# Where a turned tile's slots lie in PSUM, when the layer-2 inputs are loaded, and when lent adjacency tiles return: three edits in a four-layer graph network on one Trainium2 core

## The chip, the cores and the metric

The kernel runs on one core of one Trainium2 chip. The metric is the device time of one execution in microseconds (us); three runs give a median. The engines are named as in the profile: PE (TensorE; PEld its weight loads), DVE (VectorE), ACT (ScalarE), POOL (GpSimd) and SP (SyncE, which here only issues DMAs). ACT and POOL issue DMAs as well.

## What is computed

Four graph layers run one after the other on x (8 batches, 2048 nodes, 64 features), each followed by a residual sum and a layer norm. In short:

```python
# layer 0: hyperedge attention over H (2048 nodes x 64 edges) and a graph product
agg    = einsum('ben,bnf->bef', softmax(masked s), h)         # per hyperedge
all_he = elu(beta * h + (1 - beta) * agg)                     # per node and edge
g      = einsum('bne,benf->bnf', softmax(masked se), all_he)
industry = einsum('nm,bmf->bnf', adj / deg, x @ W_ind)
out    = mix of (industry, g) by a softmax of tanh(f @ fcW + fcb) @ av
# layer 1: normalized adjacency
H = einsum('bmd,nm->bnd', X, D^-1/2 (A + I) D^-1/2);  out = H @ W.T
# layer 2: adaptive graph convolution, supports I, adj, 2 adj adj - I and
#          apt = softmax(relu(emb @ emb.T)); weights per node from emb and weights_pool
# layer 3: three steps of a gated propagation over adj (adj_matrix), weights W1, W2
```

## The kernel before

**Layout.** Nodes lie in 16 tiles of 128 (NT) or 4 chunks of 512 (NCH, chunk c). Batches go in 4 pairs (NP, pair p). Matrix products with exact inputs are done as two matmuls, one with a rounded high part (v0h) and one with the remainder (v0l); `split` cuts them, the high part on ACT (L167) and the low part on DVE (L168). All 16 adjacency tiles stay on the core; 8 of them, 7 to 14 (LEND = 7, LENT = 8), lie in two lent blocks `adj_more`, which are written to HBM (adj_hbm) before layer 2's slots need the room, and are read back at the opening of layer 3 (`return_adj`, L1681).

**Layer 0, slot loop** (L799 to L832, 80 to 221 us). A node belongs to few hyperedges: tile t has as many "slots" as `SLOT_TILES = [16, 15, 10, 6, 3, 1, 1, ...]` has entries over t: twelve for tile 0, five for the next two, then four, three and two. For each slot PE sums pz out of three matmuls, DVE scales it (L816), ACT takes the exponential, DVE and POOL add up. `begin(t)` gathers a tile's factors into `ps`, a PSUM bank of its own (of its 512 columns 192 are used). `slots(t, ...)` turns the slot numbers of the tile after next (transpose `pslot`, two ACT copies L288) in a buffer of the rotating set "mm", which the pz tiles use too (three buffers).

**Filler.** `fill(n)` takes n matmuls out of a generator: first `products()`, the products of layer 0 with the adjacency, and then `layer1(0)` to `layer1(3)`. It is called between the steps of the slot loop (`fill(3)`, `fill(5)`) and of the mix loop, so that PE has work while other engines prepare the next step. `tick()` counts the filler matmuls; `after(n, f)` and `later(n, f)` place f that many ticks further on in the program. Where layer 1 needs a part that the program has not yet cut at that point, the generator yields "wait" and no matmul; `fill` then only ticks.

**Mix loop** (L1086 to L1105, 226 to 456 us, 16 steps i = 4p + c). A step is mix_scores, mix_end of the step before, mix_ind and mix_g of the next, and mix_weigh, each followed by fill(8) or fill(9). `mix_end` transposes (pt), normalizes and stores x1 (L971); `l1_parts(p, c)` loads it back (L992), scales it on POOL (L995) and splits it into the part that `layer1(p)` multiplies for tiles 4c to 4c + 3.

**Layer 1's end.** After each half g of a pair, `layer1` copies its two sums on ACT (ut, L1058); `l1_end` multiplies by the weights (po), normalizes and, for pairs 0 to 2, stores into x2_hbm. Once all four chunks of a pair are done and `room` is set, `load_xn` places the load of layer 2's xn[p] on ACT's queue, 14 ticks later (L1033). The instructions in `pin(...)` keep their program order on their engine; the x loads of L1033 are not pinned.

**Layers 2 and 3** follow: apt (508 to 747), the supports, 32 slots of formed weights and multiplications (to 1243), and layer 3. In slot 32 (SLOTS) the last chunk's sums are picked (DVE, L1548); then `store` sends y (L1584) and loads xb (L1590), `load` reads y back (L1596), DVE adds and normalizes (L1602, L1618), and `first_turn(3)` transposes the last quarter (pt). `load_first(NT - 4, NT - 2)` (L1634) loads tiles 12 and 13 of x from HBM.

Of the kernel before, what the change touches and what calls it, by code (L numbers as in the profile page):

```python
# [56 lines left out]
def tile_gnn_fast(  # L57
# [199 lines left out]
    def column_halves(a):  # L257
        return [a[:, cols(g, N // 2)] for g in range(2)]

    def lent_tiles():  # L260

        tiles = []
        for i in range(2):
            more = adj_pool.tile([P, LENT // 2, N], F32R, tag=f"more{i}", name="adj_more")
            tiles += [column_halves(more[:, k, :]) for k in range(LENT // 2)]
        return tiles

    adj = [adj_tile(adj_pool, t) for t in range(LEND)] + lent_tiles()

    hrows = {}  # L270

# [9 lines left out]

    def slots(t, psum, tag, bufs):

        pt = psum.tile([E, P], F32, tag=tag, name="pslot", bufs=bufs)
        transpose(pt, hrows[t][:, BF + 8:])
        slot = hy.tile([P, P], BF16, tag="slot", name="slot", bufs=2)
        for i in range(2):
            nc.scalar.copy(slot[i * E:(i + 1) * E, :], pt)  # L288
        one_hot[t] = []
        for s in range(sum(n > t for n in SLOT_TILES)):  # L290
            o = hrp.tile([P, P], F32R, tag="o", name="o", bufs=17)
            if t == 0:
                tc.keep_in_program_order(
                    nc.vector.tensor_scalar(o, slot, float(s + 1), None, op0=ALU.is_equal)
                )
            else:

                far = hy.tile([P, P], BF16, tag="far", name="far", bufs=2)
                nc.scalar.activation(far, slot, AF.Abs, bias=number[:, s:s + 1])
                nc.scalar.activation(o, far, AF.Relu, bias=1.0, scale=-1.0)  # L300
            one_hot[t].append(o)
# [463 lines left out]
    with ExitStack() as pb_scope:  # L765
        pps = pb_scope.enter_context(tc.tile_pool(name="pb_ps", bufs=1, space=PSUM))
        places["small"] = lambda shape, name: pps.tile(shape, F32, tag="mm", name=name, bufs=3)
        pl = pb_scope.enter_context(tc.tile_pool(name="pl", bufs=1))

        def begin(t):  # L770

            k = tiles.index(t)
            for ahead in tiles[k + 2:k + 4]:
                fetch_rows(ahead)
            hrow = hrows.pop(t)
            both = split(hrp, hrow[:, 0:BF], "hr", 2, [P, BF], nc.vector if t == 0 else nc.gpsimd, t == 0)
            ohs = one_hot.pop(t)
            S = len(ohs)
            ps = pps.tile([P, 12, 2, B], F32, tag="ps", name="ps", bufs=1)
            for s, o in enumerate(ohs):  # L780
                mm(ps[:, s].rearrange("p i b -> p (i b)"), lhsT=o, rhs=ts2, start=True, stop=True)

            R = pl.tile([P, 13, B], F32, tag="R", name="R", bufs=2)
            nc.vector.tensor_tensor(
                R[:, 0:S], ps[:, 0:S, 0, :], hrow[:, None, BF:BF + 8].to_broadcast([P, S, B]), ALU.add
            )
            nc.vector.tensor_reduce(R[:, S], ps[:, 0:S, 1, :].rearrange("p s b -> p b s"), AX.X, ALU.add)
            nc.vector.reciprocal(R[:, 0:S + 1], R[:, 0:S + 1])
            co = pl.tile([P, 12, B], F32, tag="co", name="co", bufs=2)
            nc.vector.tensor_tensor(  # L790
                co[:, 0:S], ps[:, 0:S, 1, :], R[:, S:S + 1, :].to_broadcast([P, S, B]), ALU.mult
            )
            return S, both, ohs, R, co


        tiles = [*range(NT - 2), NT - 1, NT - 2]
        now = begin(0)
        slots(tiles[1], pps, "mm", 3)
        for k, t in enumerate(tiles):  # L799
            S, both, ohs, R, co = now  # L800
            acc = pl.tile([P, B, F], F32, tag="acc", name="acc", bufs=2)
            for s in range(S):
                pz = pps.tile([P, C], F32, tag="mm", name="pz", bufs=3)
                for i, (l, r) in enumerate(((ident_r, both[0]), (ident_r, both[1]), (ohs[s], tab2))):
                    mm(pz, lhsT=l, rhs=r, start=i == 0, stop=i == 2)
                if s == 0 and k + 1 < NT:
                    fill(3)
                    now = begin(tiles[k + 1])
                fill(5)
                for _ in range(2):  # L810
                    if to_load:
                        load_adj(*to_load.pop(0))
                if s == max(0, S - 5) and k + 2 < NT:
                    slots(tiles[k + 2], pps, "mm", 3)
                z = pz.rearrange("p (b f) -> p b f", f=F)
                nc.vector.tensor_tensor(z, z, R[:, s, :, None].to_broadcast([P, B, F]), ALU.mult)  # L816
                y = pl.tile([P, B, F], F32, tag="y", name="y", bufs=3)
                nc.scalar.activation(y, z, AF.Exp, bias=-1.0)

                nc.vector.scalar_tensor_tensor(y, z, 1.0, y, op0=ALU.max, op1=ALU.min)  # L820
                cb = co[:, s, :, None].to_broadcast([P, B, F])
                if s == 0:
                    nc.vector.tensor_tensor(acc, y, cb, ALU.mult)
                else:
                    nc.vector.tensor_tensor(y, y, cb, ALU.mult)
                    nc.gpsimd.tensor_tensor(acc, acc, y, ALU.add)

            nc.gpsimd.indirect_dma_start(
                out=gs_hbm[:], out_offset=bass.IndirectOffsetOnAxis(ap=order[:, t:t + 1], axis=0),
                in_=acc.rearrange("p b f -> p (b f)"), in_offset=None,  # L830
            )
# [193 lines left out]

    room = []

    def load_xn():

        for p in range(NP - 1):  # L1030
            if room and done[p] == NCH:
                done[p] = 0
                after(14, lambda p=p: nc.scalar.dma_start(xn[p], x2_hbm[p][:]))  # L1033

    def layer1(p):

        for g in range(2):
            own = (2 * g, 2 * g + 1)
            ug = None
            for t in range(NT):  # L1040
                while (p, t // JT) not in part:
                    yield "wait"
                if ug is None:
                    ug = pph.tile([P, 2, C], F32, tag="ph", name="u1", bufs=2)
                    u = {c: ug[:, c % 2, :] for c in own}
                for i in range(2):
                    for c in own:
                        mm(
                            u[c], lhsT=part[p, t // JT][i][:, t % JT, :], rhs=adj_c(t, c),
                            start=t == 0 and i == 0, stop=t == NT - 1 and i == 1,  # L1050
                        )
                        tick()
                        yield
                if g == 1 and p + 1 < NP and t % JT == JT - 1:
                    l1_parts(p + 1, t // JT)
            for k, c in enumerate(own):
                ut = va.tile([P, C], F32, tag="ut", name="ut", bufs=2)
                pin(nc.scalar.copy(ut, u[c]))  # L1058
                later(6 + 8 * k, lambda p=p, c=c, ut=ut, x1=l1_load(p, c): l1_end(p, c, ut, x1))

    def all_pairs():
        yield from remaining
# [592 lines left out]

    at(SLOTS - 3, 0, first_tiles)
    at(SLOTS, 0, lambda: [first_turn(q) for q in range(3)])
    at(SLOTS, 2, lambda: load_first(NT - 4, NT - 2))
    for q in range(2):
        at(SLOTS, 1 + q, lambda q=q: factor(q, h[q], bd_e, None, True))  # L1660

    for g in range(1, SLOTS + 1):
        for period in range(4):
            for f in hooks.pop((g, period), ()):
                f()
            if 0 < g < SLOTS:
                form(g, 2 * period)
                form(g, 2 * period + 1)
            for f in picks[:2]:
                f()  # L1670
            del picks[:2]
            if g > 0:
                multiply(g - 1, period)
            if g == SLOTS:
                for f in picks:
                    f()
                picks.clear()
    store, load, *waiting = ends[-1]
    adj[LEND:LEND + LENT] = lent_tiles()

    def return_adj(tiles, eng):  # L1681
        for t in tiles:
            for g in range(2):
                pin(eng.dma_start(adj[t][g].bitcast(F32), adj_hbm[t - LEND, :, cols(g, N // 2)]))

    return_adj(range(LEND, LEND + LENT // 2), nc.gpsimd)
    store()
    load()
    return_adj(range(LEND + LENT // 2, LEND + LENT), nc.sync)


# [985 lines left out]
```

## Time and profile before

| what | value |
|---|---|
| runs | 1728.06, 1728.79, 1730.58 us; median 1728.79 |
| profiled execution | 1730.81 us; its span 1729.0, 1.8 lie around it |
| mean granted PE clock | 0.989 |
| PE busy | 1655.4 us, 96% of the span |
| DVE, ACT, POOL busy | 843.0, 589.1, 569.9 us |
| 99 to 221 us (slot loop) | PE 107.68, DVE 113.79 of 122 us |
| 242 to 454 us (mix loop) | PE 210.73, DVE 148.08 of 212 us |
| 484 to 492 us (layer 1's end) | PE 4.75 of 8 us at clock 0.57 |
| 1262 to 1275 us (layer 3's opening) | PE 7.61 of 13 us at clock 0.87 |

A row of a timeline shows start, duration, engine, line, operation, output and input, count, and in brackets the idle time before it with the instruction that ended it. A row of the waits shows who waited for whom, microseconds in total, times, and the longest one. PE's matmuls are pipelined, so their rows overlap; distances between starts are read for what one costs (one filler matmul of 512 columns: 0.233 us).

### The profile page before, as it was taken

Reading aid. Unit: us, or ns where it says so; the run is one execution under the profiler, and the core shown is the slowest. Engines: PE = TensorE matmul, PEld = TensorE weight load, DVE = VectorE, ACT = ScalarE, POOL = GpSimd, SP = SyncE. Lnnn points to the kernel's source line nnn. Section 1 sums busy time; section 2 is a strip of 40 time slices with the busy share of each in tenths; the row PEclk is TensorE's granted clock in tenths of the full one; section 3 lists DMA queues with packets and bytes.
Section 4 is the critical chain, followed back from the end, with each engine's and each line's share of the span. In section 5 each row is a group of like instructions: output and inputs, shape, how many; then the busy total and the mean of one; then the engine's idle time right before and its main releaser. Section 6 shows DMA issues by size and latency. Waiting matters only on the chain. (4 is left out here: it accounts for less than half of the span.)

```text
span 1729.0 us, 28043 instructions
## 1 busy us (share of the span) xinstructions
PE 1655.4 (96%) x11230; PEld 1208.0 (70%) x11230; DVE 843.0 (49%) x1536; ACT 589.1 (34%) x1033; POOL 569.9 (33%) x516
## 2 busy tenths in 40 slices
PE   6888899999989999999999999999989999999996
PEld 4666666666664444478888778888767877878775
DVE  7789945768742221210136157777533433433332
ACT  1355533344321212111213267878511221212221
POOL 3678845556534543422123001313210200202001
PEclk9899999999999999999999999999999999999998
DMA  9833334444330000027344457675571111211111
GB/s 341 277 134 125 121 131 138 146 147 146 117 118 1 31 31 1 24 71 296 113 134 140 118 137 158 138 168 126 171 242 48 50 55 43 62 48 42 57 43 39
DMA packets 171212, 195.83 MB, mean 113 GB/s; under 512 B 71568, under 2 KB 116368, under 8 KB 169792
## 3 DMA queue, kind: packets, MB, share of 16 engines
q1 hardware_dynamic: 160384, 154.61, 30.3%
q0 software_dynamic: 8544, 30.68, 5.3%
q10 hardware_dynamic: 2144, 8.65, 1.3%
q8 instruction: 90, 1.47, 0.4%
q14 instruction: 50, 0.41, 0.1%
HBM read 126.72 MB, written 67.17 MB: 112 GB/s over the span
## 5 line engine op out<-in xcount | busy, mean ns | idle before, releaser
L172 PE MATMUL ua<-pt,xn 128*128 128x512 f32 x512 | 230.2, 592 | 1.4 <-DVE pt L1177 1.4
L172 PEld LDWEIGHTS ua<-pt,xn 128*128 128x128 f32 x512 | 97.0, 190 | 111.0 <-issue 104.1
L1542 DVE COPY w_half<-pw 128x512 f32<-128x512 f32 x160 | 109.8, 705 | 87.8 <-PE pw L172 87.1
L1538 ACT COPY w_half<-pw 128x1024 f32<-128x1024 f32 x128 | 129.8, 1014 | 58.6 <-PE pw L172 58.5
L172 PE MATMUL py<-w_half,xg 128*32 128x128 f32 x4096 | 142.1, 279 | 3.1 <-issue 3.1
L172 PE MATMUL u<-adj,v0h 128*128 128x512 f32 (+1 forms) x388 | 135.7, 427 | 0.6 <-ACT h L1856 0.6
L172 PE MATMUL u<-adj,v0l 128*128 128x512 f32 (+1 forms) x388 | 125.8, 402 | 0.0
L172 PE MATMUL u<-adj_more,v2h 128*128 128x512 f32 (+1 forms) x388 | 125.7, 402 | 0.0
L172 PEld LDWEIGHTS py<-w_half,xg 128*32 128x32 f32 x4096 | 111.3, 138 | 20.5 <-issue 3.7
L172 PE MATMUL u<-adj_more,v2l 128*128 128x512 f32 (+1 forms) x388 | 124.0, 396 | 0.0
L1183 POOL TENSOR_TENSOR acc<-acc,pt 128x512 f32<-128x512 f32 x60 | 76.4, 1274 | 104.3 <-DVE pt L1177 103.7
L172 PE MATMUL pw<-est,wst 64*128 64x256 f32 x1024 | 109.8, 317 | 0.5 <-ACT w_half L1538 0.4
L1177 DVE TENSOR_SCALAR pt<-pt 128x512 f32<-128x512 f32 x64 | 29.8, 465 | 152.8 <-ACT pt L1176 152.7
L172 PEld LDWEIGHTS pw<-est,wst 64*128 64x128 f32 x1024 | 82.2, 185 | 25.4 <-ACT w_half L1538 18.7
L1757 ACT CAST ar<-fcav 128x512 fp32r<-128x512 f32 x64 | 39.6, 618 | 165.7 <-DMA fcav<-in_adj_t 164.8
L172 PE MATMUL u<-adj_more,v3l 128*128 128x512 f32 (+1 forms) x291 | 93.5, 396 | 2.1 <-DVE v3l L168 2.0
L1758 DVE SCALAR_TENSOR_TENSOR ar<-fcav,ar 128x512 f32<-128x512 f32 x64 | 45.6, 713 | 100.6 <-ACT ar L1757 100.6
L1176 ACT ACTIVATE pt<-s 128x512 f32<-128x512 f32 x64 | 38.0, 598 | 164.8 <-PE s L172 164.8
L172 PE MATMUL u<-adj,v1h 128*128 128x512 f32 (+1 forms) x291 | 94.0, 401 | 0.0
L172 PE MATMUL u<-adj_more,v3h 128*128 128x512 f32 (+1 forms) x291 | 93.1, 398 | 0.0
L172 PE MATMUL u<-adj,v1l 128*128 128x512 f32 (+1 forms) x291 | 92.6, 395 | 0.0
L1727 POOL TENSOR_TENSOR x<-x,rows 128x512 f32<-128x512 f32 x16 | 22.5, 1431 | 211.8 <-PE pt L175 200.5
(409 smaller groups left out, 3288.4 us busy)
## 6 DMA issues: line engine op xcount, KB each, us to landing
fcav<-in_adj_t SPq DMA_DIRECT2D x64, 256.0 KB, 2.9
u_hbm<-ut SPq DMA_DIRECT2D x48, 256.0 KB, 2.8
xg<-u_hbm SPq DMA_DIRECT2D x24, 512.0 KB, 7.0
adj<-in_adj_t POOLq DMA_DIRECT2D x16, 512.0 KB, 7.9
adj_more<-in_adj_t POOLq DMA_DIRECT2D x16, 512.0 KB, 7.9
adj_hbm<-adj_more SPq DMA_DIRECT2D x16, 512.0 KB, 6.1
x_hbm<-r SPq DMA_DIRECT2D x28, 256.0 KB, 2.3
hs_hbm<-st ACTq DMA_DIRECT2D x8, 584.0 KB, 5.9
```

The lines of the kernel that those rows point to most:

```text
L172: tc.keep_in_program_order(nc.tensor.matmul(*args, **kw))
L1176: nc.scalar.activation(pt, s, AF.Exp)
L1177: nc.vector.tensor_scalar(pt, pt, 1.0, None, op0=ALU.max)
L1183: nc.gpsimd.tensor_tensor(accs[c], accs[c], pt, ALU.add)
L1538: pin(nc.scalar.copy(dst, pw.rearrange("p j o n -> p n (j o)")))
L1542: pin(copy(dst[:, :, 2 * j:2 * j + 2], bank.rearrange("p o n -> p n o")))
L1727: nc.gpsimd.tensor_tensor(xs, xs, b2.to_broadcast([P, JT, P]), ALU.add)
L1757: nc.scalar.copy(ar, seen_a)
L1758: nc.vector.scalar_tensor_tensor(ar.bitcast(F32), seen_a, 1.0, ar.bitcast(F32), op0=ALU.mult, op1=ALU.not_equal, accum_out=left[:, t, k:k ...
```

## The change

1. **Slots.** The bank of `ps` becomes one persistent tile `shared`. For a tile with over six slots (only tile 0 has them, k = 0) the slot numbers of the tile after next are turned into its columns 384 to 511; for the others they go to an "mm" buffer as before, and `fill(4)` follows: for k = 1 to 13, 52 matmuls in all.
2. **x loads.** `load_xn` no longer places L1033's loads by ticks but collects them; `begin_loads()` issues them, on ACT's queue as before, behind the two ut copies at the end of a half of `layer1`; after the last half they are issued at once.
3. **Adjacency return.** Tiles 7 to 10 are read back on SP at the start of slot 32, in place of POOL's queue behind the slot; tiles 11 to 14 stay on SP behind `store` and `load`. `load_first(NT - 4, NT - 2)` moves from period 2 of slot 32 to behind `load`.

```diff
     def slots(t, psum, tag, bufs):
-        pt = psum.tile([E, P], F32, tag=tag, name="pslot", bufs=bufs)
+        pt = psum.tile([E, P], F32, tag=tag, name="pslot", bufs=bufs) if tag else psum
...
+        shared = pps.tile([P, C], F32, tag="ps", name="ps", bufs=1)
...
-            ps = pps.tile([P, 12, 2, B], F32, tag="ps", name="ps", bufs=1)
+            ps = shared[:, 0:24 * B].rearrange("p (s i b) -> p s i b", i=2, b=B)
...
                 if s == max(0, S - 5) and k + 2 < NT:
-                    slots(tiles[k + 2], pps, "mm", 3)
+                    if S > 6:
+                        slots(tiles[k + 2], shared[0:E, C - P:C], None, 1)
+                    else:
+                        slots(tiles[k + 2], pps, "mm", 3)
+                        fill(4)
...
+    xn_loads, at_once = [], []
+
+    def begin_loads():
+        while xn_loads:
+            p = xn_loads.pop(0)
+            nc.scalar.dma_start(xn[p], x2_hbm[p][:])
+
     def load_xn():
         for p in range(NP - 1):
             if room and done[p] == NCH:
                 done[p] = 0
-                after(14, lambda p=p: nc.scalar.dma_start(xn[p], x2_hbm[p][:]))
+                xn_loads.append(p)
+        if at_once:
+            begin_loads()
...
                 later(6 + 8 * k, lambda p=p, c=c, ut=ut, x1=l1_load(p, c): l1_end(p, c, ut, x1))
+            if (p, g) == (NP - 1, 1):
+                at_once.append(True)
+            begin_loads()
...
-    at(SLOTS, 2, lambda: load_first(NT - 4, NT - 2))
...
+    def return_first():
+        adj[LEND:LEND + LENT // 2] = lent_tiles(0)
+        return_adj(range(LEND, LEND + LENT // 2), nc.sync)
+
+    at(SLOTS, 0, return_first)
...
     store, load, *waiting = ends[-1]
-    adj[LEND:LEND + LENT] = lent_tiles()
...
-    return_adj(range(LEND, LEND + LENT // 2), nc.gpsimd)
+    adj[LEND + LENT // 2:LEND + LENT] = lent_tiles(1)
     store()
     load()
+    load_first(NT - 4, NT - 2)
     return_adj(range(LEND + LENT // 2, LEND + LENT), nc.sync)
```

`lent_tiles(i)` now makes one of the two lent blocks; `return_adj` itself is unchanged and moved up in the text.

More of the change, by code (lines that the diff above doesn't have):

```diff
@@ L258, in column_halves, with lent_tiles @@
         return [a[:, cols(g, N // 2)] for g in range(2)]
[L260 to L268, printed above, removed]
+    def lent_tiles(i):
+        more = adj_pool.tile([P, LENT // 2, N], F32R, tag=f"more{i}", name="adj_more")
+        return [column_halves(more[:, k, :]) for k in range(LENT // 2)]
+    adj = [adj_tile(adj_pool, t) for t in range(LEND)] + lent_tiles(0) + lent_tiles(1)
     hrows = {}
@@ L1657, in tile_gnn_fast, with return_adj @@
     at(SLOTS, 0, lambda: [first_turn(q) for q in range(3)])
-    at(SLOTS, 2, lambda: load_first(NT - 4, NT - 2))
     for q in range(2):
         at(SLOTS, 1 + q, lambda q=q: factor(q, h[q], bd_e, None, True))
+    def return_adj(tiles, eng):
+        for t in tiles:
+            for g in range(2):
+                pin(eng.dma_start(adj[t][g].bitcast(F32), adj_hbm[t - LEND, :, cols(g, N // 2)]))
+    def return_first():
+        adj[LEND:LEND + LENT // 2] = lent_tiles(0)
+        return_adj(range(LEND, LEND + LENT // 2), nc.sync)
+    at(SLOTS, 0, return_first)
     for g in range(1, SLOTS + 1):
@@ L1678, in tile_gnn_fast @@
     store, load, *waiting = ends[-1]
-    adj[LEND:LEND + LENT] = lent_tiles()
[L1681 to L1684, printed above, removed]
-    return_adj(range(LEND, LEND + LENT // 2), nc.gpsimd)
+    adj[LEND + LENT // 2:LEND + LENT] = lent_tiles(1)
     store()
     load()
+    load_first(NT - 4, NT - 2)
     return_adj(range(LEND + LENT // 2, LEND + LENT), nc.sync)
```

## The prediction

> **What bounds the kernel now.** The page comes first: TensorE (PE) is busy for 96% of the span, so only PE's idle time (1729.0 − 1655.4 = 73.6 us) and matmuls at a reduced clock can be won; no matmul is removed. The change touches three stretches, read by windows, waits and timelines.
>
> ```profile
> PE 1655.4 (96%) x11230; PEld 1208.0 (70%) x11230; DVE 843.0 (49%) x1536; ACT 589.1 (34%) x1033; POOL 569.9 (33%) x516
> ```
>
> Busy time by window (columns PE, PEld, DVE, ACT, POOL, then PE's clock, DMA share, GB/s):
>
> ```profile
> 110.00:123.00 13.00, 11.77 (x53) 8.83 (x53) 12.85 (x25) 7.00 (x19) 9.71 (x8) 1.00 0.14 44
> 182.00:190.00 8.00, 7.34 (x33) 5.34 (x31) 8.00 (x14) 4.91 (x12) 6.82 (x6) 1.00 0.23 60
> 242.00:454.00 212.00, 210.73 (x942) 137.50 (x941) 148.08 (x201) 86.12 (x149) 122.31 (x96) 1.00 0.41 134
> ```
>
> The slot loop (first two rows) is bound by VectorE (DVE), busy 12.85 of 13 and 8.00 of 8 us; PE has room there. In the mix loop (third row) PE has none: filler matmuls cover every latency. Two more stretches have long PE stalls. The waits at 470–510 and 1235–1290, each with sum, count and longest:
>
> ```profile
> PE po L172 <- ACT ut L1058: 3.7, 1, 3.7
> ...
> PE pt L175 <- DVE x L1618: 5.4, 2, 4.1
> PE u L172 <- DVE v3l L168: 2.0, 1, 2.0
> ```
>
> Behind the first, in ScalarE's (ACT) timeline, is a DMA issue held back and two copies queued behind it; behind the others, in the timeline of SP's queue, a chain of stores and loads:
>
> ```profile
> 486.17 0.33 ACTq L1033 DMA_DIRECT2D xn<-x_hbm  x1
> 486.61 1.07 ACT L1058 COPY ut<-u 128x512 f32<-128x512 f32 x2 [7.96 <-issue]
> ```
>
> ```profile
> 1240.89 2.09 SPq L1623 DMA_DIRECT2D x_hbm<-y  x2
> 1249.94 0.34 SPq L1634 DMA_DIRECT2D x<-x_hbm  x1
> 1250.37 3.65 SPq L1584 DMA_DIRECT2D y_hbm<-sums  x4
> 1254.07 3.17 SPq L1590 DMA_DIRECT2D xb<-xb_hbm  x2
> 1258.61 3.03 SPq L1596 DMA_DIRECT2D y<-y_hbm  x4
> 1261.74 4.58 SPq L1684 DMA_DIRECT2D adj_more<-adj_hbm  x8
> 1269.01 1.98 SPq L1623 DMA_DIRECT2D x_hbm<-y  x2
> 1271.08 2.72 SPq L116 DMA_DIRECT2D more<-in_w_t  x2
> ```
>
> [...] after 3.67 us idle at 483.5–487.2 the window 484–492 has clock 0.57. [...]
>
> **Part 1, layer-3 opening.** After slot 32 SP stands at L1634 until the store of 1240.89 has landed, 6.9 us of wait, and only at 1250.37 issues the y store, whose last sums DVE finished at 1245.6. The change moves L1634 behind the y loads, so the store can start 4.7 us sooner. The eight loads of tiles 7–10 (512 KB each, 4.44 us on POOL from 1241.80) go to SP at about 1236. At the 415 GB/s of the busy stretches 4.19 MB take 10.1 us, so they end near 1247–1248.5 and may hold the y store by up to 3; on the other hand they no longer run beside it. L1634 and tile 11 are needed by PE only at about 1264 and arrive at 1257–1261: hidden under the y chain's own 12 us; were that cover gone, L1634's 2–3 us would show. SP's eight issues (about 4.5 us) stand ahead of the 1240.89 store, which has until L1634. DVE, ACT and POOL follow the y loads as before.
> What is won: stalls 4.10 + 1.28 + 2.02 = 7.4, and about 1.4 us of half-speed matmuls at 1270–1274. The last stall also moves, as v3l (1280.69) sits on DVE behind `few`, which waited 8.39 us for `more`, last in the SP list above. So the gain equals the advance of the y chain until 8.8 us. I take −5; bounds −8.8 and +1[...].
>
> **Part 2, ScalarE's x loads.** ACT stood 8.34 us in L1033's wait for the third x2 store, with the ut copies behind it; PE lost 3.67 us at po, then 4.25 us for work of 2.29 at the low clock: 5.6 in all. With the loads in program text behind the copies this goes: −5.6. Bounds: 0 if the scheduler, which isn't bound to text order here, leaves the issue ahead of the copies; and +2 if the loads come so late (after 506) that layer 2's first matmul at 508 waits for xn: 3 MB take 7–8 us, less the 5.6.
>
> **Part 3, fill(4).** Tile 0's successor k=0 turns its slot in the free columns of ps's bank; this saves at most its part, 0.6 us, of the waits at ACT slot L288. Thirteen tiles get fill(4): 52 matmuls at 0.233 us (in the mix loop's timeline rows of two are 0.466 apart) are 12.1 us of PE work, moved forward from the mix loop.
> *In the slot loop.* From 99 to 221 PE is busy 107.7 of 122 us, so 14.3 are free, 1.2 in the 13 us of 110–123, where tiles have five slots. A fill(4) is 0.93 us, one for each tile. Tiles of five and four slots take it beside DVE's work; in the four tiles with three slots (182–190) only some 0.3–0.6 us stand free in a period of about 7, so each may grow by up to 0.7, 2.8 in all; those with two slots have more room (203–211: PE 6.70 of 8). So 12.1 − 2.8 ≈ 9 us are absorbed. Bounds: 12 if nothing grows; 6, about half, if PE's order puts each fill(4) where a pz matmul for DVE would have started.
> *In the mix loop* the 52 are missing. Layer 1 needs, for tiles 12–15 of pair p, the part that is transposed in step 4p+3 (pt), normalized, stored, loaded, scaled (L995) and split. The trace has the last two of these chains: pt at 403.93 to v3l's end at 423.4, 19.5 us, and pt at 455.69 to 476.0, 20.3. The second already has no slack: v3h's first matmul started at 475.39 and v3l's at 476.08.
>
> ```profile
> 455.69 0.66 PE L175 MATMUL pt<-ident,ind 128*128 128x128 f32 x4 [1.17 <-DVE ind L960]
> 475.39 0.63 PE L172 MATMUL u<-adj_more,v3h 128*128 128x512 f32 x2
> 476.08 0.51 PE L172 MATMUL u<-adj_more,v3l 128*128 128x512 f32 x1
> ```
>
> Counted in the code, 90, 77, 61 and 63 filler matmuls lie between pt and first use for p = 0 to 3 (check: 63 × 0.233 + 5.0 for one step's own matmuls = 19.7, as traced). With 52 done beforehand the distance falls by 52; but where the generator finds a part not yet cut at that point of the program, fill yields nothing: 2, 15 and 31 such calls up to p = 1, 2, 3. So 38, 27, 24 and 42 matmuls remain: with 5.1 us of a mix step (4.3 of bias products for p = 3) 14.0, 11.4, 10.7 and 14.1 us of PE. If the chain keeps 19.5 (20.3 for p = 3), PE stalls 5.5, 8.1, 8.8 and 6.2 = 28.6 us. But a waiting PE sends nothing to DVE, ACT and POOL, so the chain loses its queues: its own instructions with two DMA landings (2.3, 2.9) sum to 14.9 us; then the stalls are 0.9, 3.5, 4.2, 0.8 = 9.4. I take the middle, 19, and for three stalls beyond 3 us the clock loss of 1.4–2 seen above: 5. Together +24; bounds +10 and +36.
>
> **The sum** against the profiled execution (1730.8, of which 1729.0 span): −5 −5.6 −9 −0.6 +24 ≈ +4, 1735. That execution was 2.0 above the median of the runs, 1728.8, so the forecast there is 1733. The measurement of this kernel can tell about 0.2%, 3.5 us, from no change.
>
> **Rivals.**
> *A, the advance is absorbed* (faster). The chain shrinks to its own 14.9 us: mix costs 10 and the rest gives 20: about −10, 1719; with 5 gone elsewhere 1724. For it: DVE is busy only 70% of the mix loop, POOL 58%, ACT 41%. Against: the instruction order on these engines is pinned and counted in filler ticks, so the next step's work stays in the queue. It decides when stalls and clock losses stay below some 16 us.
> *B, full chain* (slower). The chain keeps 19.5–20: +36 − 20 = +16, 1745. It decides from 24 us. Against: queues of a stalled program empty.
> *C, the edits miss*: ACT's loads are issued ahead of the copies as before[...]. Each alone adds 5: 1738 with the middle mix cost. For it: L1033 isn't pinned and was issued ahead of copies that precede it in the text already. Against: if PE waits longer for (3,3), the x2 store lands in time whatever the order.
>
> **Chances.** My forecast 0.35 (its own range 1729–1739), A 0.30, B 0.20, C 0.15. No change by chance needs the mix cost to fall within 3.5 us of the 20 us gained, 16–23; a uniform cost of 10–36 puts 23% below that band, 27% in it and half above. A has more against B than a uniform cost gives it, since queues do empty, so I move faster to 0.32 and leave 0.13 within the band; slower keeps 0.55: half of the forecast's own range, C and B lie there. The range runs from A's 1718 to B's 1745; one chance in ten lies beyond either end.
>
> **What would show it.** Right: PE nearly full at 99–221 and ACT's wait of 8.3 us at 478–486 gone, the mix loop starting 2–4 us later; new PE waits of 3–9 us `u <- DVE v3l` or `ACT v3h` inside 300–480, followed by clocks under 0.9; po's 3.7 us gone; pt's wait at x L1618 gone or below 1 us, SP's y store near 1246. Wrong: no PE wait over 2 us in the mix loop (then A), or the y store still at 1250, or the slot loop longer by all 12 us, which would leave the mix loop's loss unpaid.

## The result and the profile after

| | before | changed |
|---|---|---|
| median of four runs | 1728.82 us | 1746.90 us (1744.93 to 1750.29) |
| ratio, 95% interval | | 1.0109 (1.0095 to 1.0124) |
| span of the profiled execution, mean PE clock | 1729.0 us, 0.989 | 1743.1 us, 0.984 |

The changed kernel is 18 us slower. The profiled execution of the changed kernel is the shortest of its four, that of before (1730.8 us) lies above its four, so the two traces are only 14.1 us apart; the working below divides up these 14.1.

The instants at which PE reaches the same work show where they come from:

| PE's landmark | before | changed | shift |
|---|---|---|---|
| first, last pz (slot loop) | 63.5, 219.1 | 61.7, 220.8 | −1.8, +1.7 |
| first, last pt (mix loop) | 251.4, 456.1 | 254.3, 480.6 | +2.9, +24.5 |
| first ua (layer 2) | 508.0 | 528.5 | +20.5 |
| last pw (before the opening) | 1234.1 | 1251.8 | +17.7 |
| first po of layer 3 | 1351.9 | 1366.6 | +14.7 |

The mix loop loses 21.6 us. It had been full before; now its row in the busy time by window (columns PE, PEld, DVE, ACT, POOL, PE's clock, DMA share, GB/s), with 94% clock and 22.7 us in which PE does nothing, reads:

```profile
242.00:454.00 212.00, 189.29 (x812) 120.33 (x812) 122.79 (x180) 77.26 (x132) 102.87 (x82) 0.94 0.37 125
```

PE's waits from 242 to 505 (sum, count, longest) name the cause. Before, the two longest groups were these, and the 3.7 us lay behind the mix loop:

```profile
PE po L172 <- ACT ut L1058: 5.5, 3, 3.7
PE pt L175 <- DVE ind L960: 1.2, 1, 1.2
```

In the changed kernel:

```profile
PE u L172 <- ACT v3h L167: 15.9, 3, 6.1
PE u L172 <- ACT v2h L167: 8.7, 2, 6.0
PE po L172 <- ACT ut L1070: 3.7, 2, 2.0
PE pi L172 <- ACT t L942: 1.5, 1, 1.5
PE u L172 <- DVE v3l L168: 1.3, 1, 1.3
```

PE, in `layer1`, stands before the part of tiles 12 to 15 (v3), as forecast, or of tiles 8 to 11 (v2), which the forecast did not name. Pair 2 shows both stops. The part of the second one, (2, 3), comes from the transpose at 422.09; the part of the first, (2, 2), from one at 402.96, ahead of these rows:

```profile
422.09 0.60 PE L175 MATMUL pt<-ident,ind 128*128 128x128 f32 x4
427.28 0.51 PE L172 MATMUL u<-adj_more,v2h 128*128 128x512 f32 x1 [2.73 <-ACT v2h L167]
442.35 1.22 PE L172 MATMUL u<-adj_more,v3h 128*128 128x512 f32 x2 [6.06 <-ACT v3h L167]
```

The part (2, 3) is turned at 422.09 and multiplied at 442.35, 20.3 us later. Counted as in the prediction, to the end of v3l, its chain took 21.3 us (v3l ends at 443.42), and 19.5 before. So the chain is no shorter than it was, and PE arrives early. DVE's timeline shows why PE's idleness did not shorten it:

```profile
423.68 0.69 DVE L983 SCALAR_TENSOR_TENSOR r<-pt,r 128x512 f32<-128x512 f32 x1
427.26 1.09 DVE L168 TENSOR_TENSOR v2l<-y,v2h 128x512 fp32r<-128x512 f32 x1 [2.88 <-ACT v2h L167]
428.27 0.67 DVE L879 TENSOR_REDUCE ln_m<-r 128x8 f32<-128x512 f32 x1
```

After its first step (L983, over at 424.4) the chain's mean (L879) has nothing to wait for, but it stands behind v2l of the chunk before, which waits for v2h, that is for the load and POOL step of the previous chain. DVE takes the two in this order, so one chain hangs behind the other, by 3.9 us here. DVE idles before v2l in the last step of the other pairs too: 3.4, 1.1 and 2.8 us for pairs 0, 1 and 3. The rest is a relay in which every engine waits for the one before, here SP's store of x1 and load of y, POOL's scaling and ACT's cast:

```profile
434.93 0.32 SPq L974 DMA_DIRECT2D x_hbm<-r  x1
437.47 0.42 SPq L995 DMA_DIRECT2D y<-x_hbm  x1
440.60 1.04 POOL L998 TENSOR_TENSOR y<-y,dinv 128x512 f32<-128x512 f32 x1 [3.97 <-DMA y<-x_hbm]
441.68 0.62 ACT L167 CAST v3h<-y 128x512 fp32r<-128x512 f32 x1 [4.38 <-POOL y L998]
```

Behind five of the waits PE runs at half clock; their windows (PE's clock is third from the end):

```profile
310.00:320.00 10.00, 9.10 (x28) 5.79 (x29) 3.44 (x6) 1.88 (x4) 1.84 (x2) 0.69 0.46 142
370.00:380.00 10.00, 6.64 (x20) 4.17 (x20) 4.62 (x7) 1.84 (x3) 3.92 (x3) 0.66 0.44 146
410.00:420.00 10.00, 8.89 (x38) 5.24 (x39) 4.15 (x7) 2.96 (x7) 3.63 (x3) 0.83 0.42 147
440.00:450.00 10.00, 7.65 (x25) 4.45 (x25) 4.62 (x7) 1.85 (x3) 3.91 (x3) 0.71 0.28 91
490.00:500.00 10.00, 6.00 (x18) 4.29 (x18) 5.61 (x10) 2.39 (x4) 6.15 (x5) 0.66 0.64 212
```

Windows of 0.25 us inside these stretches read 0.50, so a clock of 0.69 over 10 us is 6.2 us at half; what of that lies behind the wait's end costs half its length. Measured from the end of each wait to the return of the clock these are 5.2, 4.3, 3.4, 3.5 and 3.2 us, so about 9.8 us are lost.

In the opening of layer 3 SP's timeline now reads:

```profile
1258.53 1.37 SPq L1638 DMA_DIRECT2D x_hbm<-y  x2
1263.34 5.24 SPq L1599 DMA_DIRECT2D y_hbm<-sums  x4
1271.14 2.54 SPq L1611 DMA_DIRECT2D y<-y_hbm  x4
1273.72 0.62 SPq L1649 DMA_DIRECT2D x<-x_hbm  x1
1274.44 5.55 SPq L1679 DMA_DIRECT2D adj_more<-adj_hbm  x8
```

The y store follows the last pick (over at 1263.31) at once; before it came 4.7 us behind it. The first L1617 on DVE (L1602 in the kernel before) stands 11.5 us behind the pick in place of 17.1. From the y store to the y loads SP takes 7.8 us, 8.2 before, and the four y stores land in a median of 5.8 us, 6.7 before, so the adjacency loads ahead of it on SP do not hold it up; that they might, by up to 3 us, was an estimate of mine that no trace had shown. PE's waits at x are gone, and the one at v3l is longer:

```profile
PE u L172 <- DVE v3l L168: 3.4, 1, 3.4
```

### The profile page after: what moved, and what is told of

The parts are those of the page before. It is cut to its first block, busy times and chain, and to the rows that moved or that the text cites. A ratio compares the mean times of both kernels' runs of the same rounds, so it can differ in the third digit from the quotient of the medians.

```text
span 1743.1 us, 28024 instructions
## 1 busy us (share of the span) xinstructions
PE 1656.4 (95%) x11230; PEld 1208.6 (69%) x11230; DVE 832.2 (48%) x1536; ACT 590.7 (34%) x1033; POOL 562.8 (32%) x508
## 5 line engine op out<-in xcount | busy, mean ns | idle before, releaser
L172 PEld LDWEIGHTS py<-w_half,xg 128*32 128x32 f32 x4096 | 111.1, 138 | 17.1 <-issue 0.2
L172 PE MATMUL u<-adj_more,v3h 128*128 128x512 f32 (+1 forms) x291 | 97.0, 412 | 15.9 <-ACT v3h L167 15.9
```

The costliest lines, as they stand in the source:

```text
L172: tc.keep_in_program_order(nc.tensor.matmul(*args, **kw))
```

## The experiments

All ratios are to the kernel before, measured on the same chip; it took 1728.8 to 1730.2 us there. The runs are spread over three chips; where two of them ran on different chips, their ratios are compared. Each run has one trace.

**The three parts, one at a time.** First the changed kernel without its fill(4):

```diff
                         slots(tiles[k + 2], pps, "mm", 3)
-                        fill(4)
```

> The changed kernel without fill(4): slots in the bank of ps for tile 0, x loads and adjacency return as changed. Theory 1 (the fill(4) advance makes the whole loss, by starving the mix loop): no PE wait for v2h or v3h above 1 us between 230 and 500, po's wait of 3.7 us gone, about 1728.8 - 5.6 (ScalarE's hold) - 3 to 5 (opening) = 1718 to 1721. Theory 2 (the x loads' new place delays ScalarE's casts v2h and v3h, and that makes the waits): the waits of 4 to 6 us stay, 1735 or more.

Measured: 1726.26 us, ratio 0.9984 (0.9975 to 0.9993). The waits for v2h and v3h are gone, every one. So the move of 52 matmuls costs some 21 us, and the rest of the change (slots in the bank of ps, x loads, opening) gains 2.6, less than theory 1 had put on it, though its mechanism holds. ScalarE is still held (it stands 6.74 us before the copies of 483.72, behind an x load that waits for its store), and PE still waits for it:

```profile
PE po L172 <- ACT ut L1069: 3.9, 3, 2.5
```

The bank of ps itself loses time, too, where the prediction had a gain of 0.6 us. From the fifth slot of tile 0 to the first of tile 1 PE takes 19.9 us in all four traces with the slots as before, and 21.6 in eight of the nine with the shared bank (22.4 in the ninth). PE's waits for DVE's y from 60 to 99 us, in the kernel before and in the changed one without fill(4):

```profile
PE pz L172 <- DVE y L820: 2.4, 5, 1.1
PE pz L172 <- DVE y L822: 5.2, 6, 2.1
```

Why y comes later there, no run shows, and the rest of the change was not run with the slots as before.

Then fill(4) by itself, put into the kernel before behind `slots(...)` for k > 0:

```diff
                     slots(tiles[k + 2], pps, "mm", 3)
+                    if k:
+                        fill(4)
```

> The kernel before with fill(4) for k = 1 to 13 and nothing else. Theory 1: the mix loop shows the same four waits of 3 to 6 us for v2h and v3h as the changed kernel, with half clock behind each; without the opening's 3 us and with or without ScalarE's hold 1749 to 1756. Theory 2: slot loop gains, mix loop keeps its pace, 1720 to 1726.

Measured: 1753.37 us, ratio 1.0133 (1.0104 to 1.0162). Theory 1 holds; the waits from 242 to 505 are those of the changed kernel, so neither the x loads nor the bank of ps has a hand in them:

```profile
PE u L172 <- ACT v3h L167: 16.4, 3, 6.6
PE u L172 <- ACT v2h L167: 8.7, 2, 6.0
```

ACT isn't held by an x load in this kernel, as in the changed one, though these loads are placed as before (PE's longest wait at po is 1.9 us).

The opening alone (`return_first`, `lent_tiles(i)` and the place of `load_first` as in the change, all else as before):

> The kernel before with the adjacency return and L1634's move alone. Theory 1: y store about 5 us sooner against the last pick, pt's waits of 5.4 us gone, the wait at v3l longer (3 to 4 us) with half clock behind it: 3 us won, 1725 to 1727. Rival (the gain seen in the changed kernel's profile was the shift of two issue gaps elsewhere): 1728 to 1730. Full gain as predicted: 1724 or less.

Measured: 1725.47 us, ratio 0.9978 (0.9966 to 0.9991), 3.4 us won. The waits at x fell from 5.4 to 2.2 us, the one at v3l grew from 2.0 to 2.7:

```profile
PE u L172 <- DVE v3l L168: 2.7, 1, 2.7
PE pt L175 <- DVE x L1615: 2.2, 2, 1.3
```

The x loads alone (`xn_loads`, `begin_loads` and `at_once` as in the change, all else as before):

> The kernel before with the x loads' move alone. Theory 1: loads issued behind the ut copies, po's wait of 3.7 us and the half clock behind it gone: 5 to 6 us won, 1722 to 1724. Rival (in the changed kernel the hold went because PE's own wait let the store land in time, not by the move): the loads are issued ahead of the copies again, 1728 to 1730. Rival (loads too late): a wait of ua for xn at 508, 1730 to 1735.

Measured: 1727.48 us, ratio 0.9992 (0.9979 to 1.0004): no gain that can be told from nothing. ACT's timeline shows the load ahead of the copies that it should have followed:

```profile
485.86 0.33 ACTq L1033 DMA_DIRECT2D xn<-x_hbm  x1
486.31 1.07 ACT L1067 COPY ut<-u 128x512 f32<-128x512 f32 x2 [6.37 <-DMA x_hbm<-r]
```

So the first rival holds. The place in the program text did not bind this load, which isn't pinned.

**Pinned loads.** The changed kernel without fill(4), and:

```diff
-            nc.scalar.dma_start(xn[p], x2_hbm[p][:])
+            pin(nc.scalar.dma_start(xn[p], x2_hbm[p][:]))
```

> The changed kernel without fill(4), and with the x loads pinned to their place in the program. Theory 1 (unpinned, they were issued ahead of the copies and held ScalarE as before; pinned, they stand behind the copies): ScalarE's hold of 6.7 us, PE's wait of 2.5 us at po and the half clock go, 4 us; but they are issued at about 500 only and layer 2's first matmul waits for xn by 3 to 6 us: 1724 to 1729. Rival (enough time for the loads): 1722 to 1723.

Measured: 1729.27 us, ratio 0.9999 (0.9988 to 1.0009). Now the copies run at 482.56 and 484.44, the loads are issued from 501.77 on, and the first matmuls of layer 2 pay, as theory 1 said; the waits at po fall from 3.9 to 1.2 us:

```profile
PE ua L172 <- DMA xn<-x_hbm: 5.2, 3, 4.4
```

**Half the advance.** In the changed kernel:

```diff
-                        fill(4)
+                        fill(2)
```

> The changed kernel with fill(2) in place of fill(4): 26 matmuls ahead in place of 52. Theory 1 (the loss begins where the filler distance between a step's transpose and the use of its part becomes shorter than the chain): distances of 64 and 51 matmuls for p = 0 and 1 are enough, no wait over 1 us there; about 35 and 37 for p = 2 and 3 are not, one or two waits of 3 to 5 us each; 1730 to 1736, fewer half-clock stretches than with fill(4). Rival (each matmul moved costs the same): half of the 20.6 us, all waits half as long: 1736 to 1737.

Measured: 1736.76 us, ratio 1.0038 (1.0019 to 1.0056). PE's waits from 242 to 505:

```profile
PE u L172 <- ACT v2h L167: 6.0, 1, 6.0
PE u L172 <- ACT v3h L167: 5.0, 1, 5.0
PE pf L172 <- DVE ind L911: 2.5, 1, 2.5
```

By its waits theory 1 holds: none is left for p = 0 and 1 (longest 0.4 us), and two are left for p = 2 and 3 at nearly their full length. By its time the run can't tell the two apart: it stands 0.54% or 9.3 us above the kernel without fill(4) by the ratios (10.5 us as measured, on another chip), near half of the whole, since two further waits (this one at ind and 3.3 us at gn, at 237) came in addition.

**The same advance, and the mix loop hands it back.** In the changed kernel, fill(4) kept:

```diff
-        k = 9 if i > NCH else 8
+        k = 8 if i > NCH else 7
```

> The changed kernel, fill(4) kept, with fill(7) and fill(8) in the mix loop in place of fill(8) and fill(9), so that the mix loop hands some 60 matmuls back to the stretch behind it. Theory 1 (distance): filler distances of 52 to 73, all waits for v2h and v3h below 1.5 us, the slot loop's gain of 8 us is kept, 1717 to 1722. Rival (the mix loop's own steps need these fills): waits of PE for ACT's and DVE's results of the same step (t, th, ind) of about 1 us in most of 16 steps, 1728 to 1740.

Measured: 1722.41 us, ratio 0.9951 (0.9934 to 0.9968). With one matmul less in each fill the waits for parts go, but for one, at (3, 3); the steps' own waits stay small:

```profile
PE u L172 <- ACT v3h L167: 5.1, 1, 5.1
PE pf L172 <- DVE ind L911: 2.3, 3, 1.0
PE pt L175 <- ACT v1h L167: 2.0, 2, 1.0
```

The one at v3h is at (3, 3); one of 1.4 us at (3, 0) is left besides. The distance is not what makes the one at (3, 3): 23.9 us lie between its transpose (447.92) and PE's arrival, more than any of these chains took in the changed kernel. Here the chain took 29.0 us, as POOL stands before a sum of layer 1's end with the scaling of this part behind it:

```profile
473.77 1.41 POOL L1018 TENSOR_TENSOR r<-r,x 128x512 f32<-128x512 f32 x1 [13.35 <-DVE el L1151]
475.14 1.08 POOL L998 TENSOR_TENSOR y<-y,dinv 128x512 f32<-128x512 f32 x1
```

This kernel does the same 52 matmuls early as the changed one and stands 1.6% below it (0.9951 against 1.0109). What costs is the shorter way to the part, not the early work.

**The wait at v3l.** The changed kernel without fill(4), with:

```diff
                 for q in range(1, NP):
                     ...
-                last_constants()
...
                 factor(3, h[3], bd_e, None, True)
+                last_constants()
```

> The changed kernel without fill(4), and with last_constants() behind factor(3, ...) in the opening of layer 3, so that v3l no longer stands behind DVE's wait for the load of more. Theory 1 (v3l is late only by that wait): PE's wait of 4.2 us and the half clock behind it go, 1726.3 - 5 = 1720 to 1722. Rival (the y chain itself is what v3l waits for, or the wait moves to the bias row or fold): 1725 to 1727.

Measured: 1721.09 us, ratio 0.9954 (0.9936 to 0.9972), against 0.9984 with the constants in their place, 5 us. DVE no longer stands before `more` with v3l behind it (v3l runs at 1268.71, `few` at 1277.84), and of the opening's waits (1225 to 1320) only this one is left:

```profile
PE pt L175 <- ACT h L1498: 0.2, 1, 0.2
```

**Towards a better kernel.** Fewer mix fills and late constants together:

> The changed kernel with fill(4), one matmul less in each fill of the mix loop, and last_constants() behind factor(3, ...). If the two gains seen one by one add (each 4 to 5 us against the changed kernel without fill(4)): 1717 to 1718. If the waits in the opening take each other's place (with fewer mix fills pt waited 3.2 us for x and v3l not at all): only 0 to 2 us under the kernel with fewer mix fills, 1720 to 1722.

Measured: 1719.04 us, ratio 0.9940 (0.9927 to 0.9953). The opening has no wait over 0.2 us left; but the intervals with and without late constants overlap here, so how much of the two gains adds stays open. The wait at (3, 3) is 5.1 us, as with fewer mix fills alone. For it, another matmul less in steps 12 to 15:

```diff
-        k = 9 if i > NCH else 8
+        k = 7 if i >= 3 * NCH else 8 if i > NCH else 7
```

> As the kernel with fewer mix fills and late constants, and another matmul less in each fill of steps 12 to 15. Distance theory: 16 matmuls more lie between the last transpose and the part (3, 3), so its wait of 5.1 us shrinks by up to 3.7 us, less waits of about 1 us within the last steps: 1 to 3 us under the kernel with fewer mix fills and late constants. Rival (the steps' own waits grow by as much): the same time or more.

Measured: 1713.73 us, ratio 0.9910 (0.9896 to 0.9924), 5.3 us under the run before, more than expected. The wait at (3, 3) is gone and not only shortened: from its transpose to its use now lie 34.5 us, not 23.9. But behind a wait of 2.2 us at po PE's rows are at half pace from 458.58 to 468.31, 9.7 us (two of its 512-column matmuls take 0.86 to 1.01 us in place of 0.47), and from the last pz to the first ua this trace is only 0.3 us shorter than the one before. So the two traces don't show where the 5.3 us come from. This kernel beats both: the kernel before by 16 us on the same chip, the changed one by 2.0%. Last, fill(2) in place of fill(4), with fewer mix fills and late constants:

> As the kernel with fewer mix fills and late constants, with fill(2) in place of fill(4). Distance theory: no wait for a part at all, (3, 3) included (5.1 us and 2.6 us of half clock won), against some 4 us of slot-loop gain given up: 2 to 4 us under it or the same. Rival (what fill(4) gives in the slot loop is worth its whole 12 us): 2 to 4 us above it.

Measured: 1724.84 us, ratio 0.9973 (0.9962 to 0.9984), 5.8 us more than with fill(4), against the first expectation and beyond the rival's 2 to 4. The part (3, 3) is no longer waited for, as it said, but ACT's hold is back. From 440 to 500 PE has a single wait, and ACT's timeline shows its reason:

```profile
PE po L172 <- ACT ut L1070: 6.0, 1, 6.0
```

```profile
471.26 0.33 ACTq L1036 DMA_DIRECT2D xn<-x_hbm  x1
471.72 0.58 ACT L1070 COPY ut<-u 128x512 f32<-128x512 f32 x1
```

This wait and the one at (3, 3) take each other's place: in the changed kernel, with fill(4) alone and with fewer mix fills PE waits for a part, the x2 stores have time to land, and the loads hold no ut copy (PE's longest wait at po is 2.0 us, 1.9 us and at most 1.3). It isn't a law: in the kernel of 1713.73 us ACT is held 6.9 us, and PE loses 0.3.

The hold of 6.0 us alone does not make the 5.8, as it replaces a wait of 5.1. From the last pz to the first ua this trace is 10.4 us longer than with fill(4). Of that 6.1 are the 26 matmuls that now stand in this stretch, and 6.9 are half clock (8.4 us lost against 1.5), most of it around the hold; the waits together are 3.0 shorter. The slot loop is shorter by only 0.9. So the rival was right in this: in these two traces nearly all that the fills take into the slot loop is won there.

## Why the prediction was wrong

It was right on the direction and on where PE would wait, and too small by 14 us in the median; the measured time lies above its range. The step that failed is the length of the chain in a starved mix loop.

- *Slot loop*: "12.1 − 2.8 ≈ 9 us are absorbed". The loop grew by 3.5 us, so 8.6 were. That the sum came out is partly luck: 1.7 us of the growth lie in tile 0 and come with the bank of ps, for which −0.6 was forecast. The fills made some 2 us where 2.8 were forecast: from tile 1 on the loop took 122.5 us before and 124.4 with fill(4) alone.
- *Opening*: −5 forecast; 3.4 won when done alone, and PE's shift falls by 3.0 in the changed kernel's trace. The store came sooner by what was forecast, and PE passed v3l 5.7 us sooner, counted from the last pw. What failed is "the gain equals the advance of the y chain": PE waits 3.4 us at v3l in place of 2.0 and then runs at half clock up to 1299.4, with matmul starts 0.43 us apart in place of 0.233, which took nearly 3 us back. The prediction put the 1.4 us of half clock before among what can be won, and nothing for half clock behind v3l.
- *x loads*: −5.6 forecast, and this part alone gave 1.4 (between a gain of 3.6 and a loss of 0.7). My rival C had the reason: the loads aren't pinned and went ahead of the copies. In the changed kernel the hold is gone all the same, by the reason given there against C: PE's wait for the parts of pair 3 let the x2 store land in time (ACT's loads at 493.43, 501.74 and 506.02 have no wait for a store before them). It is gone with fill(4) alone as well, where the loads were not moved. So −5.6 and the wait at (3, 3) should not both have stood in the sum as independent terms; with fill(2) and fewer mix fills the one goes and the other comes back.
- *Mix loop*: +24, of it 19 for waits and 5 for the clock. This is the term that was mis-sized. The waits for v2h, v3h and v3l are 25.9 us (15.9 + 8.7 + 1.3), near the 28.6 of a chain of full length, and the clock took 9.8 over five waits in place of 5 over three.

The step of the mix loop that failed is "a waiting PE sends nothing to DVE, ACT and POOL, so the chain loses its queues", by which I took the middle between 14.9 and 19.5 us of chain. The distances were right: PE reached the part 14.6, 12.0 and 11.5 us of its own work behind the transpose for pairs 0 to 2, against 14.0, 11.4 and 10.7 forecast. The chain was not. To the end of v3l it took 19.7, 19.0, 21.3 and 20.8 us for pairs 0 to 3, so none came near the middle, 17.2. Before, it had taken 27.0, 24.8, 19.5 and 20.3: the first two, which had 90 and 77 matmuls of cover, did shrink, to the length of the others, and the prediction had read only the last two. What keeps the chain there is a wait that PE's idleness doesn't remove: what stands in DVE's queue ahead of a chain is not work that PE sends but the end of the previous chain, which waits itself for a load. This is read from the traces; no run changed DVE's order to test it. My rival B (full chain, 1745) came nearest, and it had 0.20.

The account in PE's time, from the last pz to ua: the shift grew by 18.8 while 12.1 us of matmuls had left this stretch, so 30.9 us were lost there. The rows give 25.9 of waits for parts, 9.8 − 2.1 = 7.7 more of half clock (2.1 before, behind the one wait of 3.67) and 3.7 − 5.5 = −1.8 at po, 31.8 in all. The forecast for the same stretch was 24 − 5.6 = 18.4. The difference of the rows to it, 13.4, is 6.9 of waits, 4.8 of clock and 1.7 of relief at ACT, which brought 3.9 (1.8 of wait, 2.1 of clock) in place of 5.6; against the 30.9 measured the rows are 0.9 too high.

Within layer 2, which no edit touches, the shift falls by 2.8 us. PE's gaps put down to issue there came to 3.1 us before and 0.9 after, without a wait in the profile; four other kernels have 1.0 to 1.3. How the runs' 18.1 and the traces' 14.1 us divide over the stretches is open too; only one trace of each was taken.

## What to carry to other kernels

Filler is a shared account: taken early where PE has room, it is missing where it spaced a producer from its consumer. Before moving it, measure how long the chain from producer to consumer takes and how much of it the filler between them covers; here the last pair had no slack at all (its v3l was ready at 476.02 and used at 476.08), and giving one matmul per fill back behind the loop (7 and 8 in place of 8 and 9) turned a loss of 1.1% into a gain of 0.5%. For the length of such a chain take the traced one, of a pair without slack, and not the sum of its own instructions: the waits of the previous chain are in it.

Look at where a late DMA issue really stands on an engine that also computes: here it went ahead of copies that precede it in the program (issued at 485.86, the first copy at 486.31), and pinned behind them it came 4.4 us too late.

## What the runs showed of the hardware that I had not expected

In these traces the length of a PE wait does not say what clock it costs. In the changed kernel, behind 2.02 us at 411.11 the window 410–420 has a clock of 0.83, 3.4 us at half speed, while around 2.73 us, which end at 427.28, the window stays at 1.00:

```profile
420.00:430.00 10.00, 7.28 (x33) 5.36 (x34) 5.97 (x9) 3.68 (x7) 5.71 (x5) 1.00 0.09 26
```

Windows of 0.25 us over 230 to 520 us show the half clock (0.50) in stretches of 3.4 and 6.8 us: one of 3.4 and four of 6.8 in the changed kernel, one of 6.8 in the kernel before. In the changed kernel they start at 309.37, 370.81, 411.76, 439.07 and 490.27, which lie 61.44, 40.95, 27.31 and 51.20 us apart, close to 18, 12, 8 and 15 times 3.41. How much idleness brings the half clock on, these traces don't show: in the kernel before it began at 484.44, 0.9 us into the wait of 3.67.

So waits of similar length have very different prices here: each of the five waits of the changed kernel cost 1.6 to 2.6 us more than itself, and the 2.2 us at po in the kernel of 1713.73 us stand before 9.7 us of rows at half pace.
